# Layer 2's experts by blocks: choice and pooling of tokens, places for the weights, and where layer 3 begins

## The chip, the cores and the metric

The kernel runs on one core of a Trainium2 chip. A core has five engines with instruction streams of their own: TensorE (PE: matrix products and transposes into PSUM), VectorE (DVE), ScalarE (ACT), GpSimd (POOL) and SyncE (SP, which here issues most DMAs). They run side by side and wait for each other through semaphores. The metric is the device time of one execution in microseconds (us). All data are fp32.

## The reference, cut to what matters

Two images of 64 x 64 tokens with 128 channels pass through four layers. Layer 0 is an attention with position terms, layer 1 a gated product over rows. Layer 2 is a causal attention without softmax (silu of squared scores, and a Toeplitz sum over positions), followed by 64 experts, each of which chooses its own tokens. Layer 3 is a softmax attention and a top-2 router over eight experts. The change lies in layer 2's experts and at the start of layer 3:

```python
t = t + _L2_attn_ref(_ln_t(t), ...)
# layer 2's experts: xn = _ln_t(t), one image at a time (4096 tokens, 64 experts, K = 8)
logits = einsum('bsd,ed->bse', xn, gate_w) + gate_b
probs = softmax(logits, axis=1)                    # over the tokens
topv, topi = top 8 tokens of each expert
pooled = einsum('bked,bke->bed', xn[topi], topv)   # one row for each image and expert
h = gelu(concat(pooled, 1) @ weight1[e])           # weight1: 64 x 129 x 512
out = concat(h, 1) @ weight2[e]                    # weight2: 64 x 513 x 128
t[topi] += out * topv
# layer 3 begins
q, k, v = linear(_ln_t(t)); t = t + softmax(q k^T / 16) v
```

## The kernel before

The tokens stay in SBUF as `x` [128, 64, 128]: 64 blocks of 128 tokens, 32 for each image. Layer 2's attention (`layer2_attn`) walks 16 blocks of 512 queries, the last of which is block 3 of the second image. For each it runs the scores and values step by step, and between the steps pieces of other jobs: the next block's queries (`prepare`), the Toeplitz sums (`positions`, matmuls of L1195), the joining of both halves with its normalisation (`join`, L1338 to L1369), the output (`output`: transposes L1403, two scaled copies L1406, two POOL products L1409, products L1414, addition to `x` L1422 and L1424), and the experts' logits (`logits`: normalisation L172, transposes L1378, copy L1380, four products through L1195, and L1385, which adds the bias, writes `pr` and takes the block's maximum). `rsqrt` (L1183 to L1188) is one ACT square root and five small DVE operations. The list of jobs sets when a piece runs; what the last block leaves over is finished after the last scores. The order in which each engine then takes the instructions is that of the built program.

`pr` [128, 4096] holds the logits with image and expert on the partitions (rows 0 to 63 the first image's) and the tokens along the row.

`layer2_ffn` then:

1. issues 16 loads of first weights on SP's queue (L1597), 1 MB each (experts e, e+16, e+32, e+48), into a pool of twelve buffers, and four loads of biases on ACT's queue (L1604, L1605);
2. chooses: exponential of whole rows with their sums (L1620), division by the sum (L1622), the eight largest (L1624), replacing them by zero in a copy (L1626), and the difference (L1627), which leaves the eight probabilities in `pr` and zero elsewhere;
3. pools: 32 transposes of `pr` (L1635) with eight copies (L1636); for each image 32 products (L1644) of the normalised tokens (64 normalisations, L172) with the transposed choice; the sum goes to `st1` (L1651), whose layout lets four experts work side by side on PE's row groups;
4. first product (L1660), bias, gelu (L1675), transposes; then 16 loads of second weights, into the same twelve buffers as they come free; second product (L1689), 32 instructions for each load;
5. bias (L1697), sorting into image order (L1700), copy (`eob`, L1708), and the outputs: for each group of four blocks and both images, products of `pr` with the results (L1719) and the addition to `x` (L1728).

All weight loads wait in SP's queue in this order; one that may not start holds up those behind it.

`layer3` then allots its space, loads the router's experts and branches on `small` (whether the scores are bounded). In the bounded branch (`l3_bounded`) the first block's statistics, square root, normalisation, transposes, `kT` copy and query products (`l3_qkv`, L1845 to L1881) come first, then the attention's steps: scores (L2076), exponentials (L2087), a running sum (L2043) and values (L2035), with the keys of the other blocks between them.

Of the kernel before, what the change touches and what calls it, by code (L numbers as in the profile page):

```python
# [8 lines left out]
F32 = mybir.dt.float32  # L9
# [5 lines left out]
P = 128  # L15
B = 2
# [23 lines left out]
class Net:  # L40
# [1037 lines left out]
    def layer2(self, kept, done, w3):  # L1078
        nc, tc, ins = self.nc, self.tc, self.ins
        with tc.tile_pool(reuse_waits="tile", name="g2", bufs=1) as gp:  # L1080
# [7 lines left out]

            pr = gp.tile([P, L], F32, tag="pr", name="f2pr")
            mx = gp.tile([P, NC // 4], F32, tag="mx", name="f2mx")  # L1090
            mv = gp.tile([P, B * NC, 2], F32, tag="mv", name="f2mv")
            r = gp.tile([P, B * NC], F32, tag="r", name="f2r")
            gate = gwT, gb, pr, mx, mv, r
            self.layer2_attn(gate, kept, w3)
            done()
            self.layer2_ffn(gate)

    def layer2_attn(self, gate, kept, w3):
# [4 lines left out]
        with ExitStack() as st:  # L1103
# [6 lines left out]
            def take(shape):  # L1110
# [18 lines left out]
            wq = self.load(wp, "wq", [P, C], ins["L2_attn_Wq"])  # L1129
            wk = self.load(wp, "wk", [P, C], ins["L2_attn_Wk"])  # L1130
            wv = self.load(wp, "wv", [P, C], ins["L2_attn_Wv"])
            wu = self.load(wp, "wu", [P, 2 * C], ins["L2_attn_Wu"])
            wf = self.load(
                wp, "wf", [P, 2, C], ins["L2_attn_Wf"].rearrange("(k p) c -> p k c", p=P)
            )
# [12 lines left out]
            gwT, gb, pr, gmx, gmv, gr = gate  # L1148
# [179 lines left out]
            def join(i):  # L1328
# [20 lines left out]
                m = 4  # L1349
                if i:  # L1350
                    m = 8
                    finish(("out", i - 1))
                    gate_stats(i - 1, var[:, 4:])
                rsqrt(r[:, :m], var[:, :m], m, f"j{i}")
                for j in range(4):
                    self.normalize(a[:, j, :], a[:, j, :], mv, r, j)
                if i:
                    n0 = at(i - 1)
                    nc.gpsimd.tensor_copy(gr[:, n0 : n0 + 4], r[:, 4:])
                    add(("gate", i - 1), 2, logits(i - 1))  # L1360
# [10 lines left out]
            def logits(i):  # L1371
# [4 lines left out]
                for j in range(4):  # L1376
# [7 lines left out]
                columns(pl[rows], gwT, xT)  # L1384
                nc.vector.tensor_scalar(  # L1385
                    pr[rows, g * 512 : (g + 1) * 512],
                    pl[rows],
                    gb[rows],
                    None,
                    ALU.add,  # L1390
                    ALU.max,
                    accum_out=gmx[rows, g : g + 1],
# [168 lines left out]
            while squared:  # L1561
                values()
            while jobs:
                finish(next(iter(jobs)))
# [4 lines left out]
            for _ in logits(last):  # L1569
                pass  # L1570


    def layer2_ffn(self, gate):
# [7 lines left out]
        with ExitStack() as st:  # L1581
            wp = st.enter_context(tc.tile_pool(reuse_waits="tile", name="f2w", bufs=1))
            ap = st.enter_context(tc.tile_pool(reuse_waits="tile", name="f2a", bufs=1))
            ps = st.enter_context(tc.tile_pool(reuse_waits="tile", name="f2p", bufs=3, space=PSUM))
            ws = st.enter_context(tc.tile_pool(reuse_waits="tile", name="f2s", bufs=12))
            _, _, pr, mx, mv, r = gate

            def weights(kind, e):

                wt = ws.tile([P, NT * WIN * NR], F32, tag="w", name=f"f2w{kind}_{e}")  # L1590
# [10 lines left out]
            b1 = wp.tile([P, FF], F32, tag="b1", name="f2b1")  # L1601
            b2 = wp.tile([P, C], F32, tag="b2", name="f2b2")
# [3 lines left out]
            st1 = wp.tile([P, NT, NR, WIN], F32, tag="st1", name="f2st1")  # L1606
            nc.gpsimd.memset(st1, 0.0)


            sort = wp.tile([P, P], F32, tag="sort", name="f2sortm")  # L1610
# [5 lines left out]

            neg = self.small.tile([P, 1], F32, tag="neg", name="f2neg")
            nc.vector.tensor_reduce(neg, mx, AX.X, ALU.max, negate=True)
            sm = self.small.tile([P, 1], F32, tag="f2sm", name="f2sm")
            nc.scalar.activation(pr, pr, AF.Exp, bias=neg, accum_out=sm)  # L1620
            nc.vector.reciprocal(sm, sm)
            nc.vector.tensor_scalar(pr, pr, sm, None, ALU.mult)  # L1622
            m8 = self.small.tile([P, 8], F32, tag="m8", name="f2m8")
            nc.vector.max(m8, pr)  # L1624
            rest = ap.tile([P, L], F32, tag="rest", name="f2rest")
            nc.vector.match_replace(out=rest, in_to_replace=m8, in_values=pr, imm_value=0.0)  # L1626
            nc.vector.tensor_tensor(pr, pr, rest, ALU.subtract)  # L1627


            prT = ap.tile([P, NC, P], F32, tag="rest", name="f2prT")  # L1630
            for g in range(NC // 4):
                pt = ps.tile([P, 4, P], F32, tag="misc", name=f"f2prT{g}")
                for i in range(4):
                    n = 4 * g + i
                    nc.tensor.transpose(pt[:, i, :], pr[:, n * P : (n + 1) * P], self.ident)  # L1635
                nc.scalar.copy(prT[:, 4 * g : 4 * g + 4, :], pt)  # L1636
            for b in range(B):
                pp = ps.tile([P, E1], F32, tag="pp", name=f"f2pp{b}", bufs=1)
                for n in range(NC):
                    if n % 4 == 0:  # L1640
                        xn = ap.tile([P, 4, C], F32, tag="xn", name=f"f2xp{b}_{n}", bufs=3)
                    at = b * NC + n
                    self.normalize(xn[:, n % 4, :], self.x[:, at, :], mv, r, at)
                    nc.tensor.matmul(  # L1644
                        pp,
# [608 lines left out]
```

## Time and profile before

| what | us |
|---|---|
| median of 3 runs | 4830.82 (4829.54 to 4831.86) |
| profiled execution | 4826.12 |
| its span, first to last instruction | 4824.3 |
| last silu of layer 2 ends | 3556.0 |
| Toeplitz sums of the last block | 3558.8 to 3571.9 |
| output of the last block: first transposes to addition to x | 3579.0 to 3588.6 |
| last logits' products | 3599.1 to 3601.0 |
| first transposes of the choice | 3622.4 |
| first product of the experts | 3643.9 |
| first scores of layer 3 | 3730.3 |

The profiled execution is 4.7 us shorter than the median of the runs. The page's first part gives each engine's busy time:

```profile
PE 4514.4 (94%) x33260; PEld 1761.8 (37%) x33260; DVE 2918.7 (61%) x4784; ACT 2661.0 (55%) x3091; POOL 945.1 (20%) x848
```

PEld is the loading of weights into PE, which overlaps its products. PE works for 94% of the span as a whole; the part that the change touches, from 3556 to 3737 us, lies in the two slices of a fortieth each in which the page shows PE busy for 7 tenths, and DMA for 2 and 5. The weights of the experts are by far the largest transfer of the kernel (columns: tile and source, queue, operation, count, KB each, us from issue to landing):

```profile
f2w<-in_L_ffn_weight_dram SPq DMA_DIRECT2D x32, 1024.0 KB, 13.1
```

In the timelines a line gives start, busy time, engine, line of the kernel, operation, output and input, count, and in brackets the idle time before it with what ended it. SPq and ACTq are the queues on which DMAs are issued; the time given there is that of issuing.

### The profile page before, as it was taken

What the parts mean: (1) busy time and instruction counts of PE and PEld (TensorE: products, weight loads), DVE (VectorE), ACT (ScalarE), POOL (GpSimd) and SP (SyncE); (2) the same over time, 40 slices, a digit from 0 to 9 for tenths busy, and PEclk for the clock granted to TensorE, in tenths of its full rate; (3) what the DMA queues carried; (4) which work ended last, traced back from release to release, by engine and by line L of the source; (5) the groups of instructions that cost most, each with busy time, mean ns of one, the idle gap of its engine ahead of it and who ended that gap; (6) DMA issues with size and microseconds to landing.
All of it is one profiled execution on the core that took longest, in us unless ns stands there. A gap on an engine that the chain in (4) does not pass through costs nothing.

```text
span 4824.3 us, 78221 instructions
## 1 busy us (share of the span) xinstructions
PE 4514.4 (94%) x33260; PEld 1761.8 (37%) x33260; DVE 2918.7 (61%) x4784; ACT 2661.0 (55%) x3091; POOL 945.1 (20%) x848
## 2 busy tenths in 40 slices
PE   6999999999999999978799999999977999999999
PEld 3333333333233333325322223322225444444443
DVE  4676767676766767766746666555553444454447
ACT  4666565655656565555667666676731444433326
POOL 1000000000000000004455454555531000000008
PEclk7999999999999999989899999999987999999999
DMA  1000000000000000000000000000025000000001
GB/s 46 10 1 10 1 10 1 10 1 10 1 1 10 1 12 1 1 6 21 6 1 1 1 1 1 1 1 1 1 93 194 1 1 0 1 0 1 0 1 36
DMA packets 43211, 60.30 MB, mean 12 GB/s; under 512 B 4352, under 2 KB 25056, under 8 KB 41696
## 3 DMA queue, kind: packets, MB, share of 16 engines
q1 hardware_dynamic: 41552, 54.34, 3.6%
q8 instruction: 265, 4.34, 0.4%
q10 hardware_dynamic: 1296, 0.82, 0.1%
q14 instruction: 98, 0.80, 0.1%
HBM read 42.56 MB, written 4.19 MB: 10 GB/s over the span
## 4 chain that ended last, share of the span: by engine, by line
PE 78%; DVE 9%; ACT 6%; POOL 3%; issue 2%; DMA 1%; SPq 0%; DVEq 0%; ACTq 0%; POOLq 0%
PE l0sc L590 17%; PE l0o L549 16%; PE scl L2076 9%; PE oTl L2035 9%; PE l2sc L1448 5%; PE l2pos L1195 5%; PE l2av L1494 3%; DVE l2es L1468 2%; PE f3ex L2185 2%; POOL l2es L1471 2%; PE l0pw L643 1%; ACT l2es L1479 1%; ACT l0es L598 1%; PE l1p L938 1%; ACT l2es L1459 1%
## 5 line engine op out<-in xcount | busy, mean ns | idle before, releaser
L601 DVE TENSOR_TENSOR l0es<-l0es,l0ew 128x1024 f32<-128x1024 f32 x1024 | 1253.4, 1228 | 586.4 <-ACT l0es L598 586.1
L598 ACT ACTIVATE l0es<-l0sc 128x1024 f32<-128x1024 f32 x1024 | 1042.8, 1024 | 676.2 <-PE l0sc L590 671.0
L549 PE MATMUL l0o<-l0es,l0v 64*33 64x512 f32 x8192 | 1068.0, 591 | 19.8 <-ACT l0os L558 12.5
L590 PE MATMUL l0sc<-l0qa,ka 64*64 64x512 f32 x8192 | 1080.6, 596 | 4.7 <-ACT l0es L598 4.7
L1479 ACT ACTIVATE l2es<-l2es 128x1024 f32<-128x1024 f32 (+3 forms) x576 | 559.5, 984 | 265.8 <-POOL l2es L1471 258.7
L1471 POOL TENSOR_TENSOR l2es<-l2es 128x1024 f32<-128x1024 f32 (+3 forms) x352 | 581.2, 1662 | 493.9 <-DVE l2es L1468 442.7
L2043 DVE TENSOR_TENSOR accl<-accl,esl 128x1024 f32<-128x1024 f32 x240 | 302.5, 1261 | 424.6 <-ACT esl L2087 421.2
L1468 DVE TENSOR_SCALAR l2es<-l2sc 128x1024 f32<-128x1024 f32 (+3 forms) x320 | 338.7, 1058 | 314.5 <-PE l2sc L1448 314.3
L2087 ACT ACTIVATE esl<-scl 128x1024 f32<-128x1024 f32 x240 | 245.6, 1023 | 485.2 <-PE scl L2076 460.1
L590 PEld LDWEIGHTS l0sc<-l0qa,ka 64*64 64x64 f32 x8192 | 294.3, 133 | 545.6 <-issue 478.4
L2076 PE MATMUL scl<-l3qT,l3kT 128*128 128x512 f32 x1024 | 487.4, 596 | 0.0
L549 PEld LDWEIGHTS l0o<-l0es,l0v 64*33 64x33 f32 x8192 | 257.2, 108 | 626.8 <-issue 559.2
L1448 PE MATMUL l2sc<-l2q,kept 32*128 32x512 f32 (+3 forms) x2304 | 391.3, 622 | 83.4 <-ACT l2es L1459 58.9
L2035 PE MATMUL oTl<-esl,l3v 128*128 128x512 f32 x960 | 451.1, 592 | 0.0
L724 POOL TENSOR_TENSOR x<-x,l0y 128x256 f32<-128x256 f32 x32 | 23.4, 731 | 2037.1 <-DVE l0y L719 1912.6
L1494 PE MATMUL l2av<-l2es,kept 128*32 128x512 f32 (+3 forms) x2304 | 312.2, 592 | 0.0
L1195 PE MATMUL l2pos<-kept 128*32 128x512 f32 x2416 | 296.8, 599 | 0.1
L2035 PEld LDWEIGHTS oTl<-esl,l3v 128*128 128x128 f32 x960 | 181.7, 190 | 225.6 <-issue 222.0
L2076 PEld LDWEIGHTS scl<-l3qT,l3kT 128*128 128x128 f32 x1024 | 188.2, 191 | 207.5 <-issue 191.3
L1459 ACT ACTIVATE l2es<-l2sc 128x1024 f32<-128x1024 f32 x224 | 226.1, 1010 | 53.2 <-PE l2sc L1448 51.8
L1448 PEld LDWEIGHTS l2sc<-l2q,kept 32*128 32x128 f32 x2304 | 116.1, 187 | 328.3 <-ACT l2es L1459 160.2
L1195 PEld LDWEIGHTS l2pos<-kept 128*32 128x32 f32 x2416 | 78.4, 111 | 175.1 <-issue 174.3
(702 smaller groups left out, 3750.0 us busy)
## 6 DMA issues: line engine op xcount, KB each, us to landing
f2w<-in_L_ffn_weight_dram SPq DMA_DIRECT2D x32, 1024.0 KB, 13.1
l0ew<-l0ew SPq DMA_DIRECT2D x16, 512.0 KB, 5.0
x<-in_x_dram SPq DMA_DIRECT2D x8, 512.0 KB, 8.9
out_dram<-x SPq DMA_DIRECT2D x16, 256.0 KB, 2.3
kept<-in_L_attn_pos_rev_dram SPq DMA_DIRECT2D x1, 1792.0 KB, 6.7
ew<-in_L_ffn_expert_w_dram SPq DMA_DIRECT2D x1, 512.0 KB, 4.0
kept<-in_L_attn_pos_rev_dram SPq DMA_DIRECT2D x1, 256.0 KB
f2b<-in_L_ffn_weight_dram ACTq DMA_DIRECT2D x2, 128.0 KB, 2.7
```

Of the source, the lines that this page charges most:

```text
L549: nc.tensor.matmul(o[64 * h : 64 * h + HD + 1, r, :], lhsT=v1[rows, k, 2 * pair + h, :], rhs=es[rows, h, :], start=(k == 0), stop=(k == NC ...
L590: nc.tensor.matmul(sc[64 * c : 64 * c + 64, h, :], lhsT=ka[rows, k0 : k0 + 64], rhs=qa[rows, k // (NC // 2), qs], start=True, stop=True,)
L598: nc.scalar.activation(es, sc, AF.Exp)
L601: nc.vector.tensor_tensor(es, es, ew[:, :, qs], ALU.mult)
L1195: nc.tensor.matmul(out[part], lhsT=lhsT[:, part], rhs=rhs, start=start, stop=stop)
L1448: nc.tensor.matmul(sc[:, h2, off:], lhsT=kT[hs, k * P : (k + 1) * P], rhs=q[hs, off:], start=True, stop=True,)
L1468: nc.vector.tensor_scalar(es[:, :, lo:], sc[:, :, lo:], root, None, ALU.mult)
L1471: nc.gpsimd.tensor_tensor(part, part, part, ALU.mult)
L1479: nc.scalar.activation(es[:, :, off:], es[:, :, off:], AF.Silu)
L1494: nc.tensor.matmul(avs[i][hs, off:], lhsT=v[:, k, hs], rhs=es[h // 2][:, h % 2, off:], start=(k == 0), stop=last,)
L2035: nc.tensor.matmul(oT, lhsT=vs[b][:, k, :], rhs=es[:, i, :], start=(k == 0), stop=(k == NC - 1),)
L2076: nc.tensor.matmul(sc[:, i, :], lhsT=kTs[b][:, k * P : (k + 1) * P], rhs=qT[:, qb * 512 : (qb + 1) * 512], start=True, stop=True,)
```

## The change

- `logits`: the bias is added alone, and a second operation writes the eight largest values of each block of 512 tokens into `best` [128, 8, 8]. 
- `choose(b)`, one image at a time: the eight largest of the 64 kept values; marks on those of `best` that are among them; then for each of eight blocks the exponential with its sum (64 x 512), a replacement of the block's marked values, and a comparison times the exponential, which writes `pr`. There is no division; the sums are kept.
- `pool(b)`: transposes to 128 x 64, copies scaled by each token's reciprocal deviation (for the second image every other group is a DVE product), and products on the unnormalised `x`; the mean over the channels is then subtracted and the sum divided out. One transposition brings both images to `st1`.
- `choose(0)` is called before the last block's jobs are finished, `pool(0)` after the last logits, and `choose(1)` and `pool(1)` step by step together.
- `join` of the last block takes two square roots of four columns in place of one of eight.
- The weights have 16 fixed places in a hand-written order of use; `st1` is the last one and is also the first `st2`. The bias loads stay on ACT's queue, after the 16 calls for first weights. The final copy is scaled by the reciprocal sum.
- The outputs run image by image; after the first image's, `l3_begin` allots layer 3's space and issues the first block's keys and queries. The branch on `small` follows after the second image's outputs.
- Layer 2's projection weights are loaded into kept space rather than into a pool.

```diff
-            gate = gwT, gb, pr, mx, mv, r
+            gate = gwT, gb, pr, best, pooled, rs, mv, r
             self.layer2_attn(gate, kept, w3)
             done()
-            self.layer2_ffn(gate)
+            self.layer2_ffn(pr, pooled, rs, begin)
...
-            wq = self.load(wp, "wq", [P, C], ins["L2_attn_Wq"])
-            wk = self.load(wp, "wk", [P, C], ins["L2_attn_Wk"])
-            wv = self.load(wp, "wv", [P, C], ins["L2_attn_Wv"])
+            wq, wk, wv = take([C]), take([C]), take([C])
+            for t, n in ((wq, "q"), (wk, "k"), (wv, "v")):
+                nc.sync.dma_start(out=t, in_=ins[f"L2_attn_W{n}"])
...
-                m = 4
-                if i:
-                    m = 8
+                if 0 < i < len(order) - 1:
                     finish(("out", i - 1))
                     gate_stats(i - 1, var[:, 4:])
-                rsqrt(r[:, :m], var[:, :m], m, f"j{i}")
+                    rsqrt(r, var, 8, f"j{i}")
+                else:
+                    rsqrt(r[:, :4], var[:, :4], 4, f"j{i}")
                 for j in range(4):
                     self.normalize(a[:, j, :], a[:, j, :], mv, r, j)
+                if i == len(order) - 1:
+                    finish(("out", i - 1))
+                    gate_stats(i - 1, var[:, 4:])
+                    rsqrt(r[:, 4:], var[:, 4:], 4, f"k{i}")
...
+                part = pr[rows, g * 512 : (g + 1) * 512]
+                nc.vector.tensor_scalar(part, pl[rows], gb[rows], None, ALU.add)
+                nc.vector.max(best[rows, g, :], part)
+                yield
...
+            def choose(b):
+
+
+                rows = slice(b * E1, (b + 1) * E1)
+                all8 = best[rows].rearrange("p g k -> p (g k)")
+                m8, neg, left = (
+                    self.small.tile([P, n], F32, tag=f"f2c{n}", name=f"f2{k}{b}", bufs=1)
+                    for k, n in (("m8", 8), ("neg", 1), ("left", 64))
+                )
+                nc.vector.max(m8[rows], all8)
+                nc.vector.tensor_scalar(neg[rows], m8[rows, 0:1], -1.0, None, ALU.mult)
+
+                nc.vector.match_replace(
+                    out=left[rows], in_to_replace=m8[rows], in_values=all8, imm_value=-3e38
+                )
+                nc.vector.tensor_tensor(left[rows], left[rows], all8, ALU.is_equal)
+                nc.vector.scalar_tensor_tensor(all8, left[rows], 1e30, all8, ALU.mult, ALU.add)
+                for g in range(NB):
+                    part = pr[rows, g * 512 : (g + 1) * 512]
+                    e = ap.tile([P, 512], F32, tag="xT", name=f"f2e{b}_{g}", bufs=3)
+                    rest = ap.tile([P, 4, C], F32, tag="xn", name=f"f2rest{b}_{g}")
+                    rest = rest.rearrange("p i c -> p (i c)")
+                    nc.scalar.activation(
+                        e[rows], part, AF.Exp, bias=neg[rows], accum_out=total[rows, g : g + 1]
+                    )
+                    nc.vector.match_replace(
+                        out=rest[rows],
+                        in_to_replace=best[rows, g, :],
+                        in_values=part,
+                        imm_value=-3e38,
+                    )
+                    nc.vector.scalar_tensor_tensor(
+                        part, rest[rows], -1e38, e[rows], ALU.is_le, ALU.mult
+                    )
+                    yield
+
+            def pool(b):
+
+
+                rows = slice(b * E1, (b + 1) * E1)
+                pp = ps.tile([P, 512], F32, tag="av", name=f"f2pp{b}", bufs=1)
+                for g in range(NB):
+                    pt = ps.tile([P, 2, 512], F32, tag="sc", name=f"f2prT{b}_{g}")
+                    pt = pt[:, 0, : 4 * E1].rearrange("p (i e) -> p i e", e=E1)
+                    for i in range(4):
+                        n = 4 * g + i
+                        nc.tensor.transpose(
+                            pt[:, i, :], pr[rows, n * P : (n + 1) * P], self.ident[rows, rows]
+                        )
+                    for i in range(4):
+                        n = b * NC + 4 * g + i
+                        if i % 2 == 0:
+                            prT = wp.tile([P, 2, E1], F32, tag="prT", name=f"f2pT{b}_{g}_{i}", bufs=3)
+                        if b == 0 or g % 2:
+                            nc.scalar.activation(
+                                prT[:, i % 2, :], pt[:, i, :], AF.Copy, scale=gr[:, n : n + 1]
+                            )
+                        elif i % 2 == 0:
+                            nc.vector.tensor_tensor(
+                                prT,
+                                pt[:, i : i + 2, :],
+                                gr[:, n : n + 2].unsqueeze(2).broadcast_to([P, 2, E1]),
+                                ALU.mult,
+                            )
+                        nc.tensor.matmul(
+                            pp[rows, :C],
+                            lhsT=prT[:, i % 2, :],
+                            rhs=self.x[:, n, :],
+                            start=(g == 0 and i == 0),
+                            stop=(g == NB - 1 and i == 3),
+                        )
+                    yield
+                mean = self.small.tile([P, 1], F32, tag="f2mean", name=f"f2mean{b}", bufs=1)
+                nc.vector.tensor_reduce(rs[rows], total[rows], AX.X, ALU.add)
+                nc.vector.reciprocal(rs[rows], rs[rows])
+                nc.vector.tensor_reduce(mean[rows], pp[rows, :C], AX.X, ALU.add)
+                nc.vector.tensor_scalar(mean[rows], mean[rows], 1.0 / C, None, ALU.mult)
                 nc.vector.tensor_scalar(
-                    pr[rows, g * 512 : (g + 1) * 512],
-                    pl[rows],
-                    gb[rows],
-                    None,
-                    ALU.add,
-                    ALU.max,
-                    accum_out=gmx[rows, g : g + 1],
+                    pooled[rows], pp[rows, :C], mean[rows], rs[rows], ALU.subtract, ALU.mult
...
             while squared:
                 values()
+            for _ in choose(0):
+                pass
             while jobs:
...
+            for _ in pool(0):
+                pass
+            chosen, sums = choose(1), pool(1)
+            for _ in chosen:
+                next(sums)
+            next(sums)
...
+            wide = [P, NT * WIN * NR]
+            places = [ws.tile(wide, F32, tag=f"w{k}", name=f"f2place{k}") for k in range(16)]
+            free = [3, 4, 5, 1, 2, 6, 7, 8, 9, 10, 11, 12, 13, 14, 0]
+
+            def place(name, keep=False):
+                k = free.pop(0)
+                if not keep:
+                    free.append(k)
+                if places[k] is not None:
+                    t, places[k] = places[k], None
+                    return t
+                return ws.tile(wide, F32, tag=f"w{k}", name=name)
+
+            def zeros(t):
+                t = t.rearrange("p (j r w) -> p j r w", j=NT, w=WIN)
+                nc.gpsimd.memset(t, 0.0)
+                return t
+
+            st1 = zeros(places[15])
...
-                wt = ws.tile([P, NT * WIN * NR], F32, tag="w", name=f"f2w{kind}_{e}")
+                wt = place(f"f2w{kind}_{e}")
...
             w1 = [weights(1, e) for e in range(NR)]
-            b1 = wp.tile([P, FF], F32, tag="b1", name="f2b1")
-            b2 = wp.tile([P, C], F32, tag="b2", name="f2b2")
             for b in range(B):
                 nc.scalar.dma_start(out=b1[b::2], in_=ins["L2_ffn_weight1"][:, C, :])
                 nc.scalar.dma_start(out=b2[b::2], in_=ins["L2_ffn_weight2"][:, FF, :])
...
+            pt = ps.tile([P, C], F32, tag="misc", name="f2poolT")
+            nc.tensor.transpose(pt, pooled, self.ident)
+            nc.vector.tensor_copy(
+                st1[:, :, :, :B], pt.rearrange("p (b j r) -> p j r b", b=B, j=NT)
+            )
...
+            st2 = [st1]
+            for c in range(1, NF):
+                st2.append(zeros(place(f"f2st2_{c}", keep=True)))
             w2 = [weights(2, e) for e in range(NR)]
...
+            nc.scalar.activation(eob, pt, AF.Copy, scale=rs)
+
+            loads.close()
+            for b in range(B):
+                rows = slice(b * E1, (b + 1) * E1)
+                for g in range(NC // 4):
+                    pt = ps.tile([P, 4, C], F32, tag="misc", name=f"f2y{b}_{g}")
+                    for i in range(4):
+                        n = 4 * g + i
                         nc.tensor.matmul(
-                            pts[b][:, i, :],
+                            pt[:, i, :],
                             lhsT=pr[rows, n * P : (n + 1) * P],
-                            rhs=eo[rows, :],
+                            rhs=eob[rows, :],
                             start=True,
                             stop=True,
                         )
-                for b in range(B):
                     xs = self.x[:, b * NC + 4 * g : b * NC + 4 * g + 4, :]
-                    nc.vector.tensor_tensor(xs, xs, pts[b], ALU.add)
+                    nc.vector.tensor_tensor(xs, xs, pt, ALU.add)
+                if b == 0:
+                    begin()
...
-            self.layer2(space, kept.close, w)
-            self.layer3(w)
-
-    def layer3(self, weights):
+            with ExitStack() as st:
+                self.layer2(space, kept.close, w, lambda: self.l3_begin(st, w))
+                self.layer3(w)
...
+    def l3_begin(self, st, w):
+
+
         nc, tc, ins = self.nc, self.tc, self.ins
         G = B * NC
...
+        wp = st.enter_context(tc.tile_pool(reuse_waits="tile", name="l3e", bufs=1, side="right"))
+        w["ones"] = wp.tile([P, 1], F32, tag="ones", name="l3ones")
+        nc.vector.memset(w["ones"], 1.0)
+        w["qT"] = wp.tile([P, L], F32, tag="qT", name="l3qT")
+        w["kT"] = wp.tile([P, L], F32, tag="kT", name="l3kT0")
+        w["vx"] = wp.tile([P, NC, C], F32, tag="vx", name="l3v0")
+        with (
+            tc.tile_pool(reuse_waits="tile", name="l3b", bufs=1) as ap,
+            tc.tile_pool(reuse_waits="tile", name="l3bps", bufs=2, space=PSUM) as ps,
+        ):
+            for _ in self.l3_qkv(ap, ps, w, 0, 0, w["qT"], w["kT"], w["vx"], "l3b"):
+                pass
...
+
+    def layer3(self, w):
...
-            for g in range(NB):
+            for g in range(1, NB):
                 jobs["keys", 0, g] = keys(0, g)
```

## The prediction

> **What bounds the kernel now.** I read the page first (span, chain by engine), then the chain of waits from 3550 us on, then the timelines of SP's and ACT's queues, then busy time by stretch. The span is 4824.3 us, and the chain is PE for 78% of it; up to 3556 us, and from 3737 us on, the change leaves PE's order as it was. The 180 us between are another matter. From the chain of waits:
>
> ```profile
> 3601.07 0.77 DVE f2pr L1385 x2
> ...
> 3602.31 3.81 ACT f2pr L1620 x2
> 3606.15 0.17 DVE f2sm L1621
> 3606.35 2.36 DVE f2pr L1622
> 3608.73 4.44 DVE f2m L1624
> 3613.26 4.50 DVE f2rest L1626 x2
> 3617.79 4.44 DVE f2pr L1627
> 3622.36 5.49 PE f2prT L1635 x32
> ...
> 3653.89 27.58 DMA f2w<-in_L_ffn_weight_dram x2
> ...
> 3688.67 14.33 DMA f2w<-in_L_ffn_weight_dram
> 3703.05 1.83 PE f2po L1689 x32
> 3704.90 0.30 DVE f2eo L1697
> ```
>
> Columns: start, length, what. From the last logits to the first transposes PE waits for 21 us of whole-row work; from 3653.89 to 3703.05 the chain is weight loads. What issues them (SP's queue, then ACT's):
>
> ```profile
> 3587.40 1.47 SPq L1597 DMA_DIRECT2D f2w<-in_L_ffn_weight_dram  x3
> 3599.02 7.82 SPq L1597 DMA_DIRECT2D f2w<-in_L_ffn_weight_dram  x6
> 3644.98 2.94 SPq L1597 DMA_DIRECT2D f2w<-in_L_ffn_weight_dram  x4
> 3595.50 0.53 ACTq L1604 DMA_DIRECT2D f2b<-in_L_ffn_weight_dram  x1
> ```
>
> One load is issued at 3556.59, three at 3587.40, the fifth not before 3599.02: 3.5 us after ACT's bias load of 3595.50. In the built program that is its only wait: DMAs take eight completion counters in turn, the fifth gets the counter of that bias load, and may not be issued before that has landed. The 13th waits for a place of the twelve (3644.98). Busy time by stretch (columns PE, PEld, DVE, ACT, POOL, PE's clock, DMA share, GB/s):
>
> ```profile
> 3571.00:3582.00 11.00, 4.20 (x24) 2.31 (x16) 9.40 (x36) 0.21 (x1) 0.75 (x2) 0.67 0.00 1
> 3582.00:3602.00 20.00, 11.89 (x40) 6.17 (x40) 9.93 (x32) 1.49 (x2) 4.06 (x4) 0.59 0.55 192
> 3602.00:3622.00 20.00, 0.00 (x0) 0.00 (x0) 18.74 (x19) 3.80 (x2) 0.00 (x0) 0.50 1.04 388
> 3625.00:3644.00 19.00, 18.16 (x153) 17.87 (x155) 13.93 (x54) 4.43 (x7) 0.00 (x0) 0.97 0.00 1
> 3662.00:3705.00 43.00, 29.06 (x516) 21.21 (x516) 1.39 (x6) 0.63 (x1) 0.00 (x0) 0.58 0.96 355
> ```
>
> DMA runs at 388 GB/s or not at all. At that rate one load (1.0486 MB) takes 2.71 us, all 32 take 87 us. So the choice and the pooling are the longest piece of work, but what the end waits for is 20 loads behind a gap.
>
> **What the Trainium skill says.** (1) "VectorE: DVE Perf Modes", the section on the TRN2 errata: an fp32 two-operand pass takes (N+151)/0.96 ns. The trace agrees: 4096 elements give 4.424, measured 4.44 (L1624, L1627). For 512 it gives 0.69, as L1422 shows (0.692). (2) "TensorE: Matmul & The Clock Gate", Part 1: a PE that isn't busy for about 3.4 us runs at half clock until it is busy again. The trace agrees: clock 0.50 while idle, 0.59 when 59% busy, 0.97 when 96% busy. (3) "ScalarE: Activation LUTs", What ACT_TABLE_LOAD costs: 1.28 us, and 1.38 of drain. The load at 3598.00 shows 1.28; no drain is seen. (4) "DMA: Bandwidth & Descriptors", Issuing engines are not separate DMA queues: SP's and ACT's transfers share the 16 engines. The trace doesn't contradict it; I take no gain from another queue.
>
> **Part by part.** I sum against the profiled execution: 4826.12 us, 4824.3 of them span. The median is 4830.82; the difference that I forecast is applied to the median.
>
> 1. *Logits in the layer-2 loop.* Each of the 16 blocks loses the fused maximum (0.756 + 0.08 read, against 0.69 for a plain add) and gains a MAX8 over 64x512, 0.69 by (1): net +0.55. In 3400 to 3540 us DVE holds 9.7% of the chain, so 13 blocks inside the loop cost 13 x 0.55 x 0.097 = +0.7; all of it on the path would be +7, none 0.
>
> 2. *First image's choice and pooling.* In the built program's order two of choose(0)'s eight blocks fall into the last scores and six beside the Toeplitz sums, which keep PE for 13.1 us (3558.8 to 3571.9); DVE is busy 2.1 and ACT 1.3 of 15 us there, so their 12 DVE passes (8 us) and 6 exps of about 0.65 fit. pool(0), 32 transposes and 64 pooling records, fills the gaps of the last output's chain, but not free of charge: ACT loads tables four times more (1.28 each; the last silus wait for POOL, so +1); the reciprocal root of the last join stands behind 12 scaled copies and one table load (+2, of 1.3 to 4); pooling records stand ahead of the last logits on PE (+3, of 1 to 5). Together δ = +6, of 3 to 12. Against it: were PE kept at full clock by the fill, the last output's records (3.3 us) and three sets of transposes and logits (1.1 and 1.9) would take half, which gives back up to 5.
>
> 3. *Second image's choice, by blocks.* It takes the place of 3602.3 to 3643.5. From the last logits at 3601.1: add 0.69, MAX8 0.69, five small operations of 0.2, so 3603.5; 16 passes of about 0.63 (that is how closely 0.69 passes follow each other) and 8 products of 0.24, so 3615.5; the last transposes 1.0 and four scaled copies 1.1; stalls between engines 1: 3618.6. PE has 32 transposes and 64 pooling records: about 0.127 each in 3622 to 3644 (20.8 us for 164), hence 12 us at full clock and 23 at half. The DVE's pace leaves it under 80% busy; I take +2, of 0 to 10. ACT's last scaled copy then ends at 3618.6 + 6 + 2 = 3626.6. The 64 normalisations (16.7 us of DVE) are gone.
>
> 4. *Weight loads.* Sixteen fixed places, 15 loads ahead of the first product in place of 12. Three can go at about 3557, two at about 3584. But the sixth has the counter of ACT's first bias load, and the four bias loads now stand behind the last scaled copy on ACT. So 27 loads wait for the end of the second image's choice: S = 3626.6 + 3.5 = 3630.1. DMA, idle from 3623 to 3647 before, is now idle ahead of that. From S on it runs without a gap: ten more places are free, and the products then free one per 1 to 2 us. Before, 20 loads from 3644.98 brought the last expert group to 3703.05: 58.1 = 20 x 2.71 + 3.9. Now 27 x 2.71 + 3.9 = 77.1, so the last group starts at 3707.2, +4.1. The products (L1660) stay hidden by the loads.
>
> 5. *Outputs and layer 3.* Before, the first result eob is made at 3705.77 and the first scores start at 3730.34: 24.6 us, of which 13.5 are outputs and 11 the first block's statistics, table load, normalisation and products, which nothing covers. Now those stand behind image 0's additions, beside image 1's outputs. DVE has 16 additions of 0.65, statistics and normalisations (about 4.5): some 15 us to the first scores, and 21 to 22 in place of 29.9 to the first values (they wait for an exp and its sum). Gain 8, of 6 to 10. Four table swaps in place of two in the first block (2.6 us) are hidden by ACT's room: 29.4 of 64 us busy in 3736 to 3800; if that cover failed, the gain would be 5.4.
>
> 6. *Weights wq, wk, wv, wf in kept space; pools by side; the If later.* Nothing: their first use at 2334.4 waits on DVE, and the loads were issued at 2313 to 2320.
>
> Sum: +0.7 + 4.1 - 8 = -3.2, so 4830.8 - 3.2 = 4827.6.
>
> **Rivals.** A measurement here can tell 0.2%, 9.7 us, from no change.
> - *PE stays at full clock (faster).* δ falls to 1 and PE's +2 to 0: S = 3623.1, the last group at 3700.2, -2.9; with +0.7 and -8 to -10 that is -10 to -12: 4820. For it: PE gets work in its gaps. Against: at 59 to 67% busy it stays slow.
> - *The counter doesn't hold the loads (much faster).* Then 15 loads are in before the products, and 17 follow from about 3628: last group 3678, -25; in all -32: 4798. For it: only a reading of the program's waits; against: 3595.50 to 3599.02 before.
> - *PE at half clock becomes the bound of the pooling, and holds back all 27 loads (slower).* δ = 12, PE +10: S = 3644.1, the last group 3721.2, +18.2; with +0.7 and -8: +10.9, 4841.7. It decides once S is later than about 3643. For it: 96 records of 0.24 are 23 us against the DVE's 12, and idle gaps between groups keep the clock low; against: at that pace PE is nearly full, which brought the clock to 0.97 in 3625 to 3644.
> - *DVE in the loop is fully on the path.* +6.3 more: +3, still within 0.2%.
>
> **How the numbers follow.** The forecast's case, including the last rival: 0.52; full clock 0.17; free loads 0.05; half clock 0.26. The likeliest's own range is 4821 to 4840. For 8 in 10 I take in full clock and half clock with its gain at the lower bound 6: 4813 to 4843. Faster 0.22, same 0.52, slower 0.26.
>
> **What would show it.** SP's sixth weight load 3.5 us after ACT's first bias load, and that after the last scaled copy; DMA idle from about 3592 to 3630, then at 388 GB/s to the last expert group; that group near 3707; first scores 15 us after eob; the last join's reciprocal root behind a table load; MAX8 of 64x512 at 0.69. The forecast falls if the sixth load is issued before 3624 or after 3643, or if the first scores follow eob by more than 19 us.

## The result, and the profile after

The changed kernel takes 4849.49 us (median of 8 runs, 4837.67 to 4852.30), the kernel before 4829.52 (8 runs, 4826.51 to 4831.86): ratio 1.0039, 95% interval 1.0028 to 1.0050, some 20 us slower. The forecast was 4827.6 with a range of 4813 to 4843.

The profiled execution has a span of 4847.9 us, 23.6 more than the one before. Both traces run through the same events, so the difference can be cut at them (us; the last column is what the forecast's steps had for the stretch):

| stretch | before | after | difference | forecast |
|---|---|---|---|---|
| start to layer 2's first scores | 2341.9 | 2343.5 | +1.7 | 0 |
| to layer 2's last values | 1214.6 | 1221.7 | +7.0 | +0.7 |
| to the end of the last logits' products | 44.5 | 44.9 | +0.4 | +6 |
| to the start of the last expert group | 102.0 | 103.2 | +1.2 | -1.9 |
| to the first output product | 3.1 | 3.6 | +0.5 | 0 |
| to layer 3's first scores | 24.2 | 32.5 | +8.3 | -8 |
| to its 33rd score record | 31.5 | 36.7 | +5.2 | 0 |
| to the end | 1062.5 | 1061.8 | -0.7 | 0 |

Two stretches hold the loss: the outputs with the start of layer 3 (+13.5), and layer 2's loop (+7.0). The chain of waits of the changed kernel (start, length, what) where it was expected to change:

```profile
3610.13 0.77 DVE f2pr L1393
...
3633.23 1.10 PE f2pp L1461 x8
...
3638.34 14.81 DMA f2place<-in_L_ffn_weight_dram
...
3698.36 14.94 DMA f2w<-in_L_ffn_weight_dram
3713.34 1.98 PE f2po L1763 x32
...
3716.95 19.31 PE f2y L1789 x92
...
3743.13 5.43 PE f2y L1789 x24
```

The choice and the pooling now take 23 us from the last logits (3610.1 to 3633.2; before, 3601.1 to 3643.5), and then weight loads lead to the last expert group, as before. New is `f2y`: before, its longest piece on the chain was 1.2 us; now 92 records alone hold it for 19.3. SP's queue and then ACT's lines, in order of time, show what held the loads:

```profile
3593.54 0.92 SPq L1713 DMA_DIRECT2D f2place<-in_L_ffn_weight_dram  x2
...
3635.47 0.92 SPq L1713 DMA_DIRECT2D f2place<-in_L_ffn_weight_dram  x2
```

```profile
3632.86 0.32 ACT L1451 ACTIVATE f2pT<-f2prT,f2r 128x64 f32<-128x64 f32 x1 [2.35 <-PE f2prT L1443]
3633.03 0.53 ACTq L1718 DMA_DIRECT2D f2b<-in_L_ffn_weight_dram  x1
```

The fourth and fifth loads go at 3593.5; the sixth waits 42 us more, until 2.4 us after ACT's first bias load, which stands among the last scaled copies. Busy time by stretch of the changed kernel (PE, PEld, DVE, ACT, POOL, PE's clock, DMA share, GB/s):

```profile
3581.00:3592.00 11.00, 9.98 (x85) 7.82 (x84) 9.45 (x40) 6.64 (x27) 1.31 (x2) 1.00 0.01 1
3610.00:3620.00 10.00, 4.49 (x22) 3.21 (x21) 8.37 (x23) 5.56 (x16) 0.00 (x0) 0.50 0.00 0
3620.00:3634.00 14.00, 13.10 (x76) 10.48 (x76) 7.17 (x19) 4.41 (x16) 0.05 (x1) 0.67 0.00 0
3671.00:3715.00 44.00, 28.06 (x520) 20.49 (x516) 1.57 (x5) 0.63 (x1) 0.82 (x3) 0.62 1.00 364
3717.00:3737.00 20.00, 20.00 (x95) 19.55 (x95) 10.43 (x29) 1.40 (x2) 1.27 (x1) 0.50 0.00 1
3737.00:3749.00 12.00, 11.54 (x41) 8.52 (x40) 3.17 (x5) 1.27 (x2) 0.00 (x0) 0.50 0.00 0
```

The fifth line is the surprise: PE is busy for 20.00 of 20 us, and its clock is 0.50 throughout. The kernel before, in the same place:

```profile
3706.00:3720.00 14.00, 12.16 (x128) 10.63 (x128) 9.61 (x16) 0.04 (x1) 0.39 (x1) 1.00 0.00 1
```

The same 128 records, 12.16 us of PE at full clock. Their form, and two pieces of the chain of waits there:

```profile
L1719 PE MATMUL f2y<-f2eob,f2pr x128: 272/272/373, 3706.1 to 3719.3; 64*128 64x128 f32 x128
```

```profile
3710.74 0.70 DVE x L1728
3711.48 0.96 PE f2y L1719 x6
```

Each record uses 64 of PE's 128 rows (64*128), and the chain goes to and fro between the additions and the next group's products.

### The profile page after: what moved, and what is told of

Its sections match the earlier page's. It is cut to its first block, busy times and chain, and to the rows that moved or that the text cites. A ratio compares the mean times of both kernels' runs of the same rounds, so it can differ in the third digit from the quotient of the medians.

```text
span 4847.9 us, 78395 instructions
## 1 busy us (share of the span) xinstructions
PE 4547.9 (94%) x33293; PEld 1780.6 (37%) x33293; DVE 2929.6 (60%) x4795; ACT 2689.3 (55%) x3171; POOL 946.0 (20%) x847
## 5 line engine op out<-in xcount | busy, mean ns | idle before, releaser
L1198 PEld LDWEIGHTS l2pos<-kept 128*32 128x32 f32 x2416 | 77.9, 111 | 173.1 <-issue 172.2
```

What stands on the lines that cost most here:

```text
L1198: nc.tensor.matmul(out[part], lhsT=lhsT[:, part], rhs=rhs, start=start, stop=stop)
```

## The experiments

### Outputs: order of the images, and where layer 3 begins

Three theories stood against each other for the 32.5 us from the first output product to the first scores: that one image at a time uses half of PE's rows (A), that PE's clock is low anyway after the weight loads (B), and that layer 3's pieces hold up the outputs (C). First, layer 3 after the outputs, images still one by one:

```diff
-                if b == 0:
+                if b == 1:
                     begin()
```

> The changed kernel with one edit: layer 3 begins after both images' outputs, which stay image by image. Three theories for the 36 us from the first result to the first scores (changed kernel 32.9 us from the start of eob to the first scores, kernel before 24.6): A, halves of PE: with one image at a time the output products use rows 0 to 63 of PE only, or 64 to 127 only, come one after the other and leave PE at half clock: 128 records x 0.21 = 27 us for the outputs here too, then 11 us for layer 3's first block: 38 us from eob to the first scores, some 4853 us in all. B, clock alone: PE is slow because of the weight loads ahead of it, whatever the order of the images: outputs 27 us as well. C, layer 3's pieces hold up the outputs in PE's queue: outputs back at 13.5 us, 24.6 us from eob to the first scores, some 4840.

Second, both images side by side in the changed kernel:

```diff
-            for b in range(B):
-                rows = slice(b * E1, (b + 1) * E1)
-                for g in range(NC // 4):
+            for g in range(NC // 4):
+                for i in range(4):
+                    n = 4 * g + i
+                    for b in range(B):
+                        rows = slice(b * E1, (b + 1) * E1)
...
-                if b == 0:
+                if g == 7:
                     begin()
```

> The changed kernel with the outputs of both images side by side as in the kernel before, and layer 3 after them. A (halves of PE): outputs 13.5 us at full clock, first scores 24.6 us after eob, and the first 32 score records after the first in 31.5 us as before, not 36.7: 13.5 us less than the changed kernel, 4836. B (clock alone): outputs stay at about 27 us, no gain, about 4850. C (layer 3's pieces in the queue): as A. With the run of image by image and layer 3 at the end, the three are told apart.

Third, the same with `g == 1`:

> The changed kernel with the outputs of both images side by side, and layer 3 begun after the second of eight groups. A: the outputs keep 13.5 us or little more, the first block's statistics, root and normalisation stand beside them, first scores about 17 us after eob: 8 us less than with layer 3 at the end, some 4828. C: layer 3's transposes and products on PE hold the outputs, which take over 20 us; first scores about 30 us after eob: some 4845. B: as in the changed kernel, about 4850.

| run | us (median) | ratio to before, 95% | outputs | to first scores |
|---|---|---|---|---|
| kernel before (trace) | | | 13.5 | 24.2 |
| changed kernel | 4849.5 | 1.0039 (1.0028 to 1.0050) | 31.6 | 32.5 |
| one by one, layer 3 after | 4849.3 | 1.0039 (1.0024 to 1.0053) | 27.0 | 31.7 |
| side by side, layer 3 after | 4831.8 | 1.0005 (0.9996 to 1.0013) | 13.1 | 17.9 |
| side by side, layer 3 after two groups | 4836.0 | 1.0015 (1.0008 to 1.0021) | 18.1 | 19.6 |

("Outputs": first product to the end of the last, us in the trace; "to first scores": from the first product.) One image at a time costs 27.0 us, 128 records of 0.21, and with layer 3's pieces among them 31.6; side by side takes 13.1 and shortens the whole by 17.5 us (4849.3 to 4831.8). So B falls, A holds. C is true to 4.6 us (31.6 against 27.0) and 5.0 (18.1 against 13.1): layer 3's pieces among the outputs delay them, though one by one the whole is no longer for it (4849.5 against 4849.3). In the run with both images side by side and `begin` called last, layer 3's first block still stands beside the outputs (its statistics run between the last additions in DVE's timeline, since only its own tokens have to be ready): the first scores come 4.8 us after the last output, not 10.7. The part of the change that was to bring 8 us does bring 6.3 (24.2 to 17.9), once the images are side by side. Of the clock, in the run one by one, and in the run side by side:

```profile
3718.00:3741.00 23.00, 23.00 (x112) 22.78 (x112) 12.08 (x32) 0.20 (x1) 1.27 (x1) 0.50 0.00 0
```

```profile
3714.00:3718.00 4.00, 3.86 (x36) 3.86 (x38) 1.75 (x6) 1.37 (x2) 0.00 (x0) 0.50 0.01 4
3721.00:3727.00 6.00, 5.49 (x62) 4.61 (x62) 5.76 (x16) 0.21 (x1) 0.00 (x0) 1.00 0.00 0
```

Both enter at 0.50. One by one stays there for 112 records without a gap; side by side is at full clock within 7 us. And in the trace of the second, most records come in pairs whose starts are 0.007 us apart. Two things are thus mixed: two halves at once, and the clock. To part them, image by image again, but each product over all 128 rows, with zeros in the other image's rows:

```diff
-                            lhsT=pr[rows, n * P : (n + 1) * P],
-                            rhs=eob[rows, :],
+                            lhsT=pr[:, n * P : (n + 1) * P],
+                            rhs=eobs[b],
```

> Image by image and layer 3 at the end, as in the run with that order, but each output product uses all 128 rows of PE: the other image's rows of the right-hand side are zero. Theory A1, PE's clock follows how much of the array works: PE is at full clock after some 5 us as with both images side by side, outputs 5 + 105 x 0.107 = 16 us in place of 27, some 4838. Theory A2, only the running side by side of two halves makes the pairs fast, and the clock stays at half: outputs 27 us again, some 4849.

Measured: 4832.5 us (ratio 1.0008, 1.0002 to 1.0015), outputs 16.7 us. In the trace the first 21 records start some 0.213 us apart, and all later ones 0.112, with no two side by side.

```profile
3714.00:3718.00 4.00, 4.00 (x20) 4.00 (x20) 1.58 (x3) 1.22 (x1) 0.00 (x0) 0.50 0.01 4
3721.00:3730.00 9.00, 9.00 (x83) 9.00 (x83) 8.28 (x22) 0.20 (x1) 1.27 (x1) 1.00 0.00 0
```

As many records, as long a queue, one after the other: only the rows at work are more, and the clock comes. So A1 holds, and not A2. The same single part of the change in the kernel before:

```diff
-            for g in range(NC // 4):
+            for b in range(B):
+                rows = slice(b * E1, (b + 1) * E1)
+                for g in range(NC // 4):
```

> The kernel before with one part of the change: outputs image by image. If half of PE's rows is what costs, the 128 output records take 27 us at half clock in place of 13.5, and layer 3 starts as late after them as before: 13.5 us more than the kernel before, 4842. Rival: in the kernel before PE comes out of the weight loads differently and warms up, outputs about 16 us, 4832.

It took 4839.2 us (ratio 1.0019, 1.0010 to 1.0028), but not evenly: of twelve runs, three lie between 4827.8 and 4829.6 and nine between 4837.5 and 4844.1. The profiled one is of the three:

```profile
3709.00:3723.00 14.00, 14.00 (x128) 13.91 (x128) 10.23 (x15) 0.00 (x0) 0.00 (x0) 1.00 0.01 1
```

Here PE's clock had risen before the first output product (it was 0.53 from 3700 to 3706 us), and 128 half-row records kept it for 14.0 us. So half the rows held a full clock, but did not raise a low one in 27 to 32 us. One by one at full clock, the outputs take 14.2 us, only 0.7 more than in the kernel before: the 27 us need both, no pairs and the low clock. That the nine longer runs entered at half clock fits their 9 to 15 us and their lower mean clock (0.956 to 0.958, against 0.960 to 0.962 in the three), but no trace shows one of them. In all traces of the changed kernel and its variants the outputs begin at half clock, in all traces of the kernel before and its variants at full clock; what decides that was not tested.

### Weight loads: the counter

```diff
-                nc.scalar.dma_start(out=b1[b::2], in_=ins["L2_ffn_weight1"][:, C, :])
-                nc.scalar.dma_start(out=b2[b::2], in_=ins["L2_ffn_weight2"][:, FF, :])
+                nc.sync.dma_start(out=b1[b::2], in_=ins["L2_ffn_weight1"][:, C, :])
+                nc.sync.dma_start(out=b2[b::2], in_=ins["L2_ffn_weight2"][:, FF, :])
```

> The changed kernel with one edit: the four bias loads of the experts on SP's queue, behind the first weights, in place of ACT's. Counter theory: the sixth weight load then waits for no bias load, is issued at about 3592 us and not at 3638, 14 loads are in at about 3620, and 18 remain from about 3632: 18 x 2.71 + 4.8 = 53.6, so the last expert group starts near 3686 in place of 3713, some 27 us less: 4822. Rival, the fixed places hold the loads: they come free one by one as the first products end, the sixth load is earlier but the last group starts after 3705: 4841 or more.

4827.7 us, 21.8 less than the changed kernel (ratio to the kernel before 0.9998, 0.9989 to 1.0006). The last expert group starts at 3690.9 in place of 3713.3. The loads of this run, SP's queue, and busy time by stretch:

```profile
3593.02 1.79 SPq L1713 DMA_DIRECT2D f2place<-in_L_ffn_weight_dram  x3
```

```profile
3595.00:3617.00 22.00, 10.52 (x56) 5.63 (x52) 16.77 (x50) 6.24 (x16) 1.48 (x1) 0.71 1.03 382
3620.00:3632.00 12.00, 11.41 (x66) 9.26 (x65) 7.17 (x19) 3.52 (x13) 0.00 (x0) 0.65 0.39 143
```

The sixth load is the second of these three, at 3593.6 where it was 3635.5, and DMA runs at 382 GB/s beside the choice, where the changed kernel had none. So it was the bias loads on ACT's queue that had held the sixth load, and the 26 behind it; that the link between them is a shared counter is read from the built program, and no trace shows it. The gain is 5 us short of the forecast 27: the fifteenth load still waits for the choice on DVE (3631.3), and DMA falls to 143 GB/s ahead of it. The same edit in the kernel before:

> The kernel before with the bias loads on SP's queue. Its twelve buffers are full long before the first product (DMA idle from 3623 to 3647 us), so the fifth load is issued some 10 us earlier, at about 3589, DMA is idle for longer, and the 20 loads behind the products end as before: 4829, no change. Rival: the kernel before loses time to the same wait, and gains over 8 us.

4828.0 us, no change (0.9997, 0.9988 to 1.0006), though the fifth load goes at 3592.0 in place of 3599.0: there the wait cost nothing, since the twelve buffers are taken early in any case (the twelfth load goes at 3609.3, and the thirteenth waits for a place until 3648.0). Both gains together:

> Both edits that gained, together: bias loads on SP's queue, outputs of both images side by side, layer 3 after them. If the two gains are independent (21.8 us and 17.7 us against the changed kernel's 4849.5): 4810, faster than the kernel before by 19. Rival: what one edit frees the other loses again (layer 3's weights and PE's clock are met earlier), then 4820 or more.

4808.9 us (ratio 0.9961, 0.9947 to 0.9974). The gains add: 40.6 us from the changed kernel, where the two alone bring 21.8 and 17.7.

### Layer 2's loop: the maxima

```diff
+                nc.vector.max(self.best[rows, g, :], pr[rows, g * 512 : (g + 1) * 512])
                 yield
```

> The kernel before with one MAX8 of 64x512 more in each block's logits, whose result nothing reads. Theory: the extra maxima are what layer 2's loop lost: 16 x 0.69 us of DVE work, partly on the path, so the last values end about 6 us later than in the kernel before's trace (3556.5), steps of 3 us at about 2811 and 3042 us: 4835 us. Rival: the kernel before's one trace had luck with PE's clock there, and the maxima cost under 2 us: no such steps against a second trace of the kernel before, 4830 or less.

> The kernel before itself, for a second trace. If its first trace is typical, the last values of layer 2 end within 1 us of 3556.5 after allowing for the start. If it had luck, they end about 3 us later, with a step at about 2811 us.

From layer 2's first scores to its last values, in us (the image order and the place of the bias loads come after the loop and leave it as it is):

| traces | loop |
|---|---|
| kernel before, twice | 1214.6, 1215.0 |
| kernel before, outputs image by image | 1215.1 |
| kernel before, bias loads on SP's queue | 1216.1 |
| kernel before with the maxima | 1219.5 |
| changed kernel | 1221.7 |
| seven of its variants | 1220.4 to 1220.6 |

No trace without the maxima comes near those with all sixteen: in the kernel before they cost 3.4 to 4.9 us of loop time, of the 7.0. In total time they cost 4837.8 against 4829.1 (ratio 1.0019, 1.0012 to 1.0026); the trace is that of the fastest of the twenty runs (4831.6), so where the others lose some 6 us more is not seen. The second trace of the kernel before starts layer 2 3.9 us later, and from there on runs nearly as the first: such shifts ahead of layer 2 come and go from run to run, and the +1.7 of the table above is one of them.

Against the first trace of the kernel before, the changed kernel loses most of its loop time in two steps, near 2811 and 3042 us. They are another matter: neither of them needs the maxima. The one near 2811 us (3.3 us) also stands in the trace of the kernel before with the bias loads on SP's queue, and the one near 3042 (3.4 us) in that with the outputs image by image. What sets the traces with all sixteen maxima apart is that every one of them has both. Busy time of the same 12 us: second trace of the kernel before, kernel before with maxima, kernel before with the bias loads on SP's queue:

```profile
2807.00:2819.00 12.00, 9.99 (x76) 5.33 (x80) 7.85 (x10) 5.09 (x7) 4.58 (x4) 0.86 0.00 1
```

```profile
2803.00:2815.00 12.00, 11.32 (x56) 5.76 (x56) 5.04 (x7) 3.62 (x4) 3.17 (x3) 0.57 0.00 1
```

```profile
2806.00:2818.00 12.00, 11.38 (x56) 5.76 (x56) 5.05 (x7) 3.59 (x4) 3.13 (x3) 0.57 0.01 1
```

After the same idle gap (3.08 us in the first, 3.09 in the others) PE comes back to full clock after some 4 us in the first, and 11 in the other two, with the maxima and without. To see which maxima matter, the first image's eight were moved, in the version with both gains, from the loop to the head of `choose(0)`:

```diff
-                nc.vector.max(best[rows, g, :], part)
+                if b:
+                    nc.vector.max(best[rows, g, :], part)
...
+                for g in range(NB if b == 0 else 0):
+                    nc.vector.max(best[rows, g, :], pr[rows, g * 512 : (g + 1) * 512])
```

> The version with both gains (bias loads on SP's queue, both images' outputs side by side, layer 3 after them; 4808.9 us), with the first image's eight MAX8 taken out of layer 2's loop and put at the head of its choice, beside the last Toeplitz sums. If the maxima of the loop caused its loss, the steps of 3 us near 2811 and 3042 us vanish, the last values of layer 2 end 3 to 5 us earlier (counted from layer 2's first scores), and the choice, 5 us of DVE longer, stays hidden: 4804. Rival: the steps come from PE's clock alone and stay whatever the maxima: 4809 to 4812.

4802.0 us, ratio 0.9947 (0.9933 to 0.9961), the fastest version here, though its interval overlaps that of the version it comes from. Four of its five runs are shorter than every run of that version; its trace is that of the fifth. The loop takes 1216.8 in place of 1220.6; the step near 3042 is gone, the one near 2811 is not. So taking the first image's maxima out of the loop goes with 3.8 us less of it. That they cause the step near 3042 is not shown: this trace has the pattern of steps of the kernel before with the bias loads on SP's queue (1216.1), which has no maxima at all. The step near 2811 is PE's clock after a gap; what decides its length stays open. On the chain of waits of this version the experts still wait for loads, and the outputs have become short:

```profile
3633.22 15.68 PE f2ph L1740 x128
...
3651.75 14.04 DMA f2w<-in_L_ffn_weight_dram
...
3688.70 1.98 PE f2po L1766 x32
...
3692.30 2.13 PE f2y L1794 x16
```

### Layer 3's first block

```diff
-            for _ in self.l3_qkv(ap, ps, w, 0, 0, w["qT"], w["kT"], w["vx"], "l3b"):
-                pass
+            for g in range(2):
+                for _ in self.l3_qkv(ap, ps, w, 0, g, w["qT"], w["kT"], w["vx"], "l3b"):
+                    pass
```

> The version with both gains, with layer 3's first two blocks of keys beside the outputs in place of one. If the four swaps of ACT's table in the first attention block (two before) are what makes the first 32 score records take 34.9 us in place of 31.5, one swap less gains 1.3 to 2.6 us: 4807. Rival: the second block's work on DVE delays the first scores by as much: 4809 to 4812.

4812.5 us: no gain, as the rival had it. From the first output product to the first scores it took 21.7 us, where the version it comes from took 16.8. The attention's first steps (34.5 us to the 33rd score record) were as long as in that version (34.9; before 31.5). ACT loads a table seven times in them, nine times in that version and five times in the kernel before, at 1.28 us each: two loads fewer brought nothing. Nor is it the clock: in the trace of the version with both gains it is 1.00 throughout these steps. What makes them 3 us longer stays open.

## Why the prediction was wrong

*What bounds the kernel, and step 4 (weight loads): right.* 27 loads from S, the issue of the sixth, took 77.9 us (3635.5 to 3713.3), forecast 77.1; the sixth load follows ACT's bias load; S came at 3635.5 where 3630.1 was forecast: the start and the loop put in 8.7 us, and the steps up to S gave back 3.3 of them. The rival of free loads, which was given 0.05, is in its mechanism what one edit makes of this kernel, at 4827.7 us in place of 4798.

*Step 2 (δ = 6): wrong in size, 0.4.* With pool(0) in its gaps PE stood at clock 1.00 from 3581 to 3592, as the faster rival had it; that this gave back what table load, copies and records cost is likely, but they were not measured one by one. *Step 3 (choice of the second image): 23.6 us* from the last logits to ACT's last copy, forecast 19.5: here PE did run at 0.50 and then 0.67; if all of the excess is its doing, it cost 6 rather than 2. The two misses, -5.6 and +4.1, nearly cancel: that the two steps and the loads together made +1.6, where +4.1 was forecast, is in part luck. The slower rival rested on this stretch: its 4841.7 is nearer to the measured time than the forecast, but its place was the wrong one.

*Step 5 (outputs and layer 3): the step that failed, by 21.5 us of the sum (-8 to +13.5).* It counted the DVE's 16 additions (16 x 0.65 = 10.4 us) as the pace of the outputs, put PE's products at nothing, and did not ask what the new order does to PE: "DVE has 16 additions of 0.65, statistics and normalisations (about 4.5): some 15 us to the first scores". The 128 products had stood as 64 pairs on two halves of PE; one by one at half clock they are 27 us, and with layer 3's pieces 31.6. The first scores follow eob by 32.9 us, where more than 19 was named as the sign that the forecast falls. The form of the tile, 64 rows, stood in the trace's lines before, and so did the overlap of many of the records. It also put layer 3's pieces at no cost to the outputs (they cost 4.6 us), and had the table swaps "hidden by ACT's room". The first steps took 5.2 us more, and some 3 more in the versions with early scores too; two loads fewer did not shorten them, and their cause stays open.

*Step 1 (maxima in the loop): mis-sized, and priced by the wrong measure.* +0.7 was forecast; 3.4 to 4.9 is measured for the maxima alone (0.69 us more in each block, where the change adds 0.55 net by the prediction's estimate), and 7.0 in all, of which the variants with the same loop show 5.8 to 6.0. The share that DVE holds of the chain in one window (9.7%) was taken as the price of more DVE work. The loop does not answer in proportion: most of its loss stands in two steps of some 3 us (at the one near 2811 PE waits and then works at half clock), and which of them occur differs between traces even without the maxima. That the bound named there, +7, is the measured 7.0 is luck: it stood for DVE work that is wholly on the path, which no run shows.

Between the forecast's -3.2 and the trace's +23.6 lie 26.8 us: 21.5 of step 5, 6.3 of step 1 and 1.7 of the start, less 2.5 that the chain and the loads came out shorter; the small stretches before the first output and at the end cancel to 0.2.

## What to carry to other kernels

Before splitting a loop over two operands that sit on different rows of PE, look whether their records overlap in the trace: the pair is one pass and the halves are two, here at a clock that did not rise in 27 to 32 us. Where loads share completion counters, look at what stands between the issue of each and the counter that it waits for, on every queue; here small loads on a busy engine's queue held up 27 large ones, and whether that cost anything depended on how many buffers were free. The share of an engine on the chain prices the work that is there, not work that is added. And a step in one trace is not an effect of the edit until traces without the edit lack it.

## What the runs showed of the hardware

PE's clock doesn't follow PE's busy time alone. With 64 of 128 rows at work, PE was busy for 23.00 of 23 us at clock 0.50; with 128 rows it reached full clock after 21 records (4.4 us); with two halves side by side within 7 us; and 64 rows kept a full clock for 14.0 us. The Trainium skill ("TensorE: Matmul & The Clock Gate", Part 1: The HAM clock gate) says that the clock rises after about 3.4 us of sustained activity: for full rows the runs are near it (4.4 us), for half rows at half clock they don't agree, and the measurement decides. Its page "TensorEngine Tiling (Array Packing)", Key Properties, says that different tiles of PE can work in parallel: the pairs, 0.007 us apart, agree. Nor is the time back to full clock one number: after a gap of 3.1 us in layer 2 it was some 4 us in one trace and 11 in two others.
